# Another order of the 32 blocks in layers 1 to 3 of a sparse graph network

## The chip, the cores and the metric

The kernel runs on one core of one Trainium2 chip. The metric is the device time of one execution in microseconds. The core has several engines that run side by side, each with its own queue of instructions in program order: TensorE (PE, with its weight loads PEld), VectorE (DVE), ScalarE (ACT), GpSimd (POOL) and SyncE (SP, which here only issues DMAs). Semaphores order them where one needs another's result.

## The reference

Input `x` has 4096 rows of 256 numbers, and `adj` is a 4096 x 4096 matrix of zeros and ones, symmetric, with ones on the diagonal and few others (a row has some ten). Four layers follow one another, each of the form

```
h = relu(layernorm(x));   x = x + attention_l(h, adj)
```

Layer 0 is a graph attention with 4 heads: a row's score for a neighbour is a sum of two scalars behind a leaky ReLU, softmax runs over the neighbours, the values are `h @ W`, and an ELU follows. Layer 1 has one head, and adds `h @ W` too. Layer 2 has 4 heads and a bias. Layer 3 is dot attention with 4 heads, `softmax(q k / 8) v`, over the neighbours. A row needs the rows of all its neighbours, so no row of a layer can be worked on before all rows of the layer before are done, wherever its neighbours stand.

## The kernel before

The first stage (`lists`, some 430 us) reads `adj`, finds each row's neighbours, sorts the rows by their number of neighbours, and writes them to DRAM in that order. From then on the rows stand in 32 blocks of 128, block 0 with the rows of most neighbours. `CAPS[b]` is the number of neighbours, or slots, that block b is given (lines 40 to 43):

```
CAPS = [
    23, 14, 13, 12, 12, 11, 11, 10, 10, 10, 9, 9, 9, 9, 9, 8,
    8, 8, 8, 7, 7, 7, 7, 6, 6, 6, 6, 5, 5, 5, 4, 3,
]
```

They sum to 277. The fallback of `Net`, a dense version behind a test at the end, isn't taken here.

Each layer l reads a table in DRAM, `tab[l]`, with one row for each row of `x`. For a block, POOL issues one indirect DMA for each slot (`fetch`, line 757): 128 rows of the table, one for each partition, into one slot of `s_ring` in SBUF. The ring holds 36 x 512 numbers: 64 slots of 288 in layer 1, 69 of 264 in layer 2, 36 of 512 in layer 3. In layers 2 and 3 a block of odd K takes one slot more.

`layer` (lines 808 to 902) goes through the blocks in the order of the list `order`: `FIRST` in layer 0, `ORDER` in layers 1 to 3. In round i it does this, and each engine gets its part of it in this order:

- `fill(i)` issues the fetches of coming blocks, up to four blocks ahead (`AHEAD`). A block is placed behind the last one in the ring, or at its start, and only if these slots aren't held by a block that is not yet worked off in program order; otherwise filling stops until the next round. In layer 3 it also stops when four blocks are held, and each block brings a load of its own value rows (`s_vself`, line 834) on SP's queue.
- `norm(d)` finishes the layernorm of an earlier block d for the next layer and turns it on PE (line 742).
- `scores(b)` makes the scores of block b = order[i] on DVE and their exponentials on ACT (line 957). It begins at lines 917 and 918 in layers 1 and 2, and at lines 937 and 940 (products and sums over 256 columns for every slot) in layer 3. In layer 1 `mutual` (from line 965) belongs to it.
- `third(e)` finishes the table row of a still earlier block (`advance`: lines 1098 and 1099 for table 2, 1105 to 1115 for table 3, whose DMA is line 1106), and issues what lies in `made`: in layer 3 the output rows of the block of two rounds before, as an indirect DMA on POOL (`send`, line 767).
- `product(d)` multiplies block d's turned rows with the next layer's weights on PE (line 750).
- `weigh(b)` sums the neighbours' values. In layer 1 DVE does it alone, one instruction for each slot (lines 1008 and 1010). In layers 2 and 3 DVE multiplies up to eight slots at once (line 1039), and PE sums two slots in each pair of matmuls with the identity (line 1044; line 1032 for the block's own row where K is even, after line 1024 has halved its weight).
- `settle(c)` adds the sum to `x` and starts the next layernorm: for the block itself in layer 1, for the block of the round before in layers 2 and 3 (lines 1078 and 571 to 587; in layer 3 only lines 1068 and 1069, which make the output row).

After the last round the last blocks are carried through the same steps, without other work beside them. The first fetch of the next layer waits until the last row of its table is written.

`ORDER` before takes blocks from both ends in turn: 0, 31, 1, 30, 2, 29 and so on, with 14, 17, 15, 16 last. `FIRST` begins with 31, 30, 29, 28, 0, and also sets in which order `reload` brings in the rows; it isn't touched.

Of the kernel before, what the change touches and what calls it, by code (L numbers as in the profile page):

```python
# [47 lines left out]

WL = W + TOPK

ORDER = [b for k in range(16) for b in (k, 31 - k)]

FIRST = [31, 30, 29, 28, 0] + [b for k in range(1, 14) for b in (28 - k, k)] + [14]

# [17 lines left out]
class Sparse:  # L72
# [735 lines left out]
    def layer(self, l):  # L808
# [5 lines left out]
        ring = self.ring[:, : slots * wide].rearrange("p (k w) -> p k w", w=wide)  # L814
        order = ORDER if l else FIRST
        todo, held, at = list(order), {}, 0
# [870 lines left out]
```

## Time and profile before

| | us |
|---|---|
| median of 9 runs | 1817.63 |
| lowest and highest run | 1814.46, 1823.91 |
| the profiled execution | 1819.06 |
| its span, first to last instruction | 1817.3 |
| first fetch of layer 0 | 431.18 |
| first fetch of layers 1, 2, 3 | 643.15, 1014.03, 1388.92 |
| last fetch of layer 3 begins | 1789.72 |
| last send of layer 3 begins | 1811.69 |

| engine | busy us | share of the span |
|---|---|---|
| DVE | 1384.8 | 76% |
| POOL | 1185.4 | 65% |
| PE | 982.1 | 54% |
| ACT | 423.9 | 23% |

The profile is one execution. A row of its timeline gives the start in us, the duration in us, the engine, the line of the kernel, the operation with the tile that it writes and those that it reads, and, in brackets, how long the engine stood idle before it and what ended that. [...] The fetches are known to a block by counting: the order of the blocks is in the code, and K fetches belong to each. In layer 1 the form of line 965 tells the block's K (its second size is 23 x K), and in layers 2 and 4-head scores generally line 918's second size is 4 x K.

### The profile page before, as it was taken

What the parts mean: (1) busy time and instruction counts of PE and PEld (TensorE: products, weight loads), DVE (VectorE), ACT (ScalarE), POOL (GpSimd) and SP (SyncE); (2) the same over time, 40 slices, a digit from 0 to 9 for tenths busy, and PEclk for the clock granted to TensorE, in tenths of its full rate; (3) what the DMA queues carried; (4) which work ended last, traced back from release to release, by engine and by line L of the source; (5) the groups of instructions that cost most, each with busy time, mean ns of one, the idle gap of its engine ahead of it and who ended that gap; (6) DMA issues with size and microseconds to landing.
All of it is one profiled execution on the core that took longest, in us unless ns stands there. A gap on an engine that the chain in (4) does not pass through costs nothing. (4 is left out here: it accounts for less than half of the span.)

```text
span 1817.3 us, 14342 instructions
## 1 busy us (share of the span) xinstructions
PE 982.1 (54%) x2551; PEld 473.5 (26%) x2551; DVE 1384.8 (76%) x3900; ACT 423.9 (23%) x1240; POOL 1185.4 (65%) x1324
## 2 busy tenths in 40 slices
PE   4877877752576602223222167788684354454455
PEld 2523323221454401111111033334341121121112
DVE  6888999952689808888888168888885587887886
ACT  5864434101244401111111012222221000000000
POOL 1067756676666267777776577777773577776774
PEclk9988989875688955555555589899987676677777
DMA  9899887347633144444444345454444577775773
GB/s 329 279 395 336 303 276 253 102 140 243 187 98 95 46 102 123 133 130 132 130 132 113 74 119 137 131 135 133 134 131 124 154 214 208 207 208 176 210 203 112
DMA packets 123017, 312.89 MB, mean 172 GB/s; under 512 B 31236, under 2 KB 49671, under 8 KB 122920
## 3 DMA queue, kind: packets, MB, share of 16 engines
q0 software_dynamic: 68064, 207.46, 40.9%
q1 hardware_dynamic: 54856, 104.44, 16.6%
q14 instruction: 73, 0.60, 0.1%
q8 instruction: 24, 0.39, 0.1%
HBM read 276.80 MB, written 35.00 MB: 172 GB/s over the span
## 5 line engine op out<-in xcount | busy, mean ns | idle before, releaser
L757 POOL DMA_INDIRECT s_ring<-s_tab,s_near x924 | 883.8, 956 | 348.0 <-issue 185.6
L1044 PE MATMUL s_acc<-s_ring,s_ident 128*128 128x512 f32 x588 | 313.0, 686 | 184.2 <-issue 93.3
L757 POOL DMA_INDIRECT s_g<-s_tab,s_keep x192 | 183.1, 954 | 64.4 <-issue 58.0
L1044 PEld LDWEIGHTS s_acc<-s_ring,s_ident 128*128 128x128 f32 x588 | 127.5, 223 | 363.7 <-issue 242.2
L485 DVE MAX8 s_cand<-s_pt 128x8 f32<-128x256 f32 x512 | 181.8, 417 | 17.7 <-PE s_pt L483 17.3
L1039 DVE TENSOR_TENSOR s_ring<-s_ring,s_shares 128x2048 f32<-128x2048 f32 (+7 forms) x121 | 187.5, 1573 | 0.0
L742 PE MATMUL s_pht<-s_ident,s_h 128*128 128x128 f32 x128 | 34.4, 361 | 250.2 <-ACT s_h L734 250.1
L750 PE MATMUL s_ps<-s_we_l,s_ht 128*128 128x264 f32 x256 | 114.7, 592 | 93.0 <-ACT s_ht L744 93.0
L1010 DVE SCALAR_TENSOR_TENSOR s_acc<-s_ring,s_p,s_acc 128x256 f32<-128x256 f32 x277 | 135.7, 490 | 9.7
L263 ACT ACTIVATE s_low<-s_raw 128x1024 fp8e4<-128x1024 int32 x128 | 134.2, 1049 | 22.6 <-DMA s_raw<-in_adj_dram 19.7
L558 PE MATMUL s_ae<-s_g,s_ident 128*128 128x512 f32 x192 | 116.1, 701 | 37.2 <-DVE s_g L549 37.2
L478 PE MATMUL s_pt<-s_low,s_mark 128*128 128x512 fp8e4 x256 | 108.7, 425 | 32.5 <-DVE s_cand L485 12.8
L577 ACT ACTIVATE s_y<-s_mv,s_eps 128x1 f32<-128x1 f32 x96 | 28.3, 294 | 390.3 <-DVE s_mv L572 390.3
L750 PE MATMUL s_ps_kv<-s_wkv,s_ht 128*128 128x512 f32 x128 | 80.7, 763 | 67.1 <-ACT s_ht L744 67.1
L937 DVE TENSOR_TENSOR s_ring<-s_ring,s_shares 128x2048 f32<-128x2048 f32 (+7 forms) x48 | 81.1, 1690 | 36.2 <-DMA s_ring<-s_tab,s_near 35.7
L483 PE MATMUL s_pt<-s_places,s_stands 128*128 128x512 bf16 x256 | 107.5, 420 | 1.4 <-DVE s_stands L455 1.4
L957 ACT ACTIVATE s_shares<-s_e 128x32 f32<-128x32 f32 (+8 forms) x87 | 17.5, 201 | 376.7 <-DVE s_e L950 376.7
L918 DVE TENSOR_TENSOR s_e<-s_ring,s_rx 128x8 f32<-128x8 f32 (+12 forms) x87 | 15.8, 181 | 113.9 <-DMA s_ring<-s_tab,s_near 109.7
L750 PEld LDWEIGHTS s_ps<-s_we_l,s_ht 128*128 128x128 f32 x256 | 63.8, 276 | 124.0 <-ACT s_ht L744 114.0
L742 PEld LDWEIGHTS s_pht<-s_ident,s_h 128*128 128x128 f32 x128 | 18.1, 172 | 291.3 <-ACT s_h L734 279.8
L940 DVE TENSOR_REDUCE s_e<-s_ring 128x32 f32<-128x2048 f32 (+7 forms) x48 | 81.2, 1692 | 1.7
L502 POOL TENSOR_SCALAR s_ids<-s_top 128x23 f32<-128x23 f32 x32 | 10.1, 314 | 108.6 <-DVE s_top L493 108.3
(195 smaller groups left out, 1690.2 us busy)
## 6 DMA issues: line engine op xcount, KB each, us to landing
s_raw<-in_adj_dram SPq DMA_DIRECT2D x128, 512.0 KB, 8.3
s_ring<-s_tab,s_near POOLq DMA_INDIRECT x924, 3.0
s_rx<-s_placed SPq DMA_DIRECT2D x32, 262.0 KB, 7.3
s_tab<-s_kv SPq DMA_DIRECT2D x32, 256.0 KB, 2.9
s_tab<-s_keep SPq DMA_DIRECT2D x8, 528.0 KB, 7.7
s_tab<-s_rx SPq DMA_DIRECT2D x32, 132.0 KB, 2.1
s_keep<-in_x_dram SPq DMA_DIRECT2D x8, 512.0 KB, 8.3
s_vself<-s_tab SPq DMA_DIRECT2D x32, 128.0 KB, 3.6
```

The lines of the kernel that those rows point to most:

```text
L263: nc.scalar.activation(low[r][:, ts(h, n // 4)], raw.pop(q), AF.Copy, saturate=False, accum_out=self.sums[:, r, h : h + 1],)
L478: nc.tensor.matmul(pt, lhsT=self.mark, rhs=lo[:, ts(g, IB)], start=True, stop=False)
L483: nc.tensor.matmul(pt, lhsT=self.stands[:, g, :], rhs=self.places, start=False, stop=True)
L485: nc.vector.max(out=cand[:, g * (IB // CH) + k, :], in_=pt[:, ts(k, CH)])
L558: nc.tensor.matmul(acc, lhsT=self.ident, rhs=g[:, :, k, 0:D], start=False, stop=(k == E - 1))
L750: self.nc.tensor.matmul(ps[:, :width], lhsT=ht[:, c, :], rhs=w[:, c, :], start=(c == 0), stop=(c == KC - 1),)
L757: return self.nc.gpsimd.indirect_dma_start(out=out, out_offset=None, in_=table[:, :], in_offset=bass.IndirectOffsetOnAxis(ap=idx, axis=0),)
L937: nc.vector.tensor_tensor(kq, kq, q.unsqueeze(1).to_broadcast([P, m, D]), ALU.mult)
L940: nc.vector.tensor_reduce(e[:, k0 : k0 + m, :], kq.rearrange("p k (h d) -> p k h d", h=4), AX.X, ALU.add)
L1010: nc.vector.scalar_tensor_tensor(acc, g[:, k, 0:D], p[:, k, :], acc, ALU.mult, ALU.add)
L1039: nc.vector.tensor_tensor(v, v, p[:, k0 : k0 + m, :].unsqueeze(3).to_broadcast([P, m, H, D // H]), ALU.mult)
L1044: nc.tensor.matmul(both, lhsT=self.ident, rhs=g[:, k : k + 2, v0 : v0 + D], start=(k == 0 and not full), stop=(k + 2 >= K),)
```

## The change

The list `ORDER` is replaced. Nothing else is changed.

```
-ORDER = [b for k in range(16) for b in (k, 31 - k)]
+
+ORDER = [0, 1, 2] + [b for k in range(3, 15) for b in (30 - k, k)] + [15, 28, 29, 30, 31]
+assert sorted(ORDER) == list(range(32))
```

Layers 1, 2 and 3 now take blocks 0, 1, 2 first (23, 14 and 13 slots), then 27, 3, 26, 4, 25, 5 and so on down to 16, 14, and at the end 15, 28, 29, 30, 31 (8, 5, 5, 4 and 3 slots). The first block is the same. Layer 0 keeps its order.

## The prediction, made before the changed kernel was run

> **What bounds the kernel now.** I read the table of busy time by stage, then POOL's timeline where each layer begins and ends, then DVE's waits by layer, then DVE's timeline for single blocks. All ahead of 643 us uses FIRST and stays. First the stages, one row each for the fetches of layers 1, 2 and 3:
>
> ```profile
> core 0: us, PE busy (x) PEld busy (x) DVE busy (x) ACT busy (x) POOL busy (x), PEclk, DMA share, GB/s
> 643.00:992.00 349.00, 84.47 (x180) 43.92 (x180) 274.07 (x935) 50.27 (x182) 264.02 (x277) 0.50 0.49 128
> 1014.00:1364.00 350.00, 247.10 (x600) 119.34 (x601) 256.94 (x747) 75.56 (x261) 265.09 (x277) 0.87 0.49 128
> 1389.00:1791.00 402.00, 186.03 (x306) 71.37 (x306) 306.17 (x436) 21.40 (x91) 290.20 (x304) 0.72 0.68 198
> ```
>
> No engine is at 9 tenths, yet 277 fetches take 349 us: each needs 0.95 us and 0.30 us of issue, 1.257 us in all, and in layers 1 and 2 they stand without a hole. POOL's timeline at the ends of layers 1 and 2:
>
> ```profile
> 990.34 0.95 POOL L757 DMA_INDIRECT s_ring<-s_tab,s_near  x1 [0.30 <-issue]
> 1014.03 0.95 POOL L757 DMA_INDIRECT s_ring<-s_tab,s_near  x1 [22.74 <-DMA s_tab<-s_rx]
> ...
> 1362.30 0.95 POOL L757 DMA_INDIRECT s_ring<-s_tab,s_near  x1 [0.30 <-issue]
> 1388.92 0.95 POOL L757 DMA_INDIRECT s_ring<-s_tab,s_near  x1 [25.67 <-DMA s_vself<-s_tab]
> ```
>
> So a layer is 277 fetches and a drain of 22.7 or 25.7 us, in which DVE finishes what it has in hand and the last table rows are written. The order decides what DVE has in hand. DVE's waits, layer 1 and then layer 2:
>
> ```profile
> DVE s_e L918 <- DMA s_ring<-s_tab,s_near: 37.8, 1, 37.8
> ...
> DVE s_e L918 <- DMA s_ring<-s_tab,s_near: 59.0, 17, 36.1
> ```
>
> In layer 1 DVE waits once for a fetch, for block 0, and never again: from 677.2 to 1007 it is the slower of the two. In layer 2 it waits 17 times, so it is level with POOL. What a block costs DVE is read from one block's start to the next's (L965 in layer 1; L917 in layer 2):
>
> ```profile
> 736.54 0.33 DVE L965 TENSOR_SCALAR s_eq<-s_ring,s_own_f 128x115 bf16<-128x115 f32 x1
> 744.80 0.36 DVE L965 TENSOR_SCALAR s_eq<-s_ring,s_own_f 128x276 bf16<-128x276 f32 x1
> ...
> 987.56 0.31 DVE L965 TENSOR_SCALAR s_eq<-s_ring,s_own_f 128x184 bf16<-128x184 f32 x1
> 997.45 0.31 DVE L965 TENSOR_SCALAR s_eq<-s_ring,s_own_f 128x184 bf16<-128x184 f32 x1
> ...
> 1119.39 0.15 DVE L917 TENSOR_TENSOR s_e<-s_rx 128x4 f32<-128x4 f32 x1
> 1127.70 0.16 DVE L917 TENSOR_TENSOR s_e<-s_rx 128x4 f32<-128x4 f32 x1
> ```
>
> A block of 5 slots costs DVE 8.26 us in layer 1 and 8.31 in layer 2; POOL fetches it in 5 x 1.257 = 6.3. A block of 8 costs 9.9 against 10.1: level. So small blocks burden DVE, large ones POOL, and their place in the order matters.
>
> **The change, part by part.** No instruction is added or removed: the same 831 fetches, matmuls and vector operations are issued, only permuted, those on SP too (the table writes and the loads of s_vself follow their blocks).
>
> *Layer 1, the end.* Now the last five blocks are 15, 28, 29, 30, 31 with 8, 5, 5, 4, 3 slots. Before, small blocks early gave DVE a store of work; with 0, 1, 2 first (50 fetches) and the small ones last, it runs dry. Without a wait DVE would reach block 14 at 34.0 (its start in the layer) + 330.2 (all its blocks, 677.2 to 1007.4) - 51.8 (the last six) = 312.4 us into the layer; block 14 lands at 252 x 1.257 + 2.0 = 318.8. So it waits there, and then holds the end: blocks 14, 15, 28, 29, 30 cost 10.6 (9 slots, 967.02 to 977.58) + 9.9 + 8.3 + 8.3 + 7.7 (4 slots, 716.13 to 723.82) = 44.7 us, while POOL fetches the 25 slots after block 14 in 31.4. Block 31 begins 13.3 us after it landed; block 16 now begins 4.2 after (landed 993.2, begun 997.4). That is +9.1; the last block itself costs 7.1 (3 slots, 695.75 to 702.83) in place of 9.9, -2.8. **Sum +6.3 us.** Bounds: 3 if the drain hides half, 9 if the 2.8 is lost on PE or ACT.
>
> *Layer 2, the end.* DVE is at its landing when block 15 comes. Blocks 15, 28, 29, 30 cost 9.4 (8 slots, 1355.20 to 1364.45 and 0.13 to L918) + 8.3 + 8.3 + 8.2 (4 slots, 1078.72 to 1086.93) = 34.2 us; POOL's 17 fetches take 21.4. Block 31 begins 12.8 after landing; block 16 began 0.2 after: +12.6. Its own chain is shorter: L1039 0.95 in place of 2.28, L1024 gone (0.2), a wait of 0.96 for PE before L1078 gone: -2.5. **Sum +10.1.** Four small blocks in a row are not in this trace. Bounds: 5, half of it, since each small block stands beside a large one now and some of its 8.3 may be theirs; and 25, if PE becomes the limit (rival three).
>
> *Layer 3, the beginning.* Its ring has 36 slots. Blocks 0 and 31 fill 28; block 1 waits until PE has read block 0:
>
> ```profile
> 1420.37 0.95 POOL L757 DMA_INDIRECT s_ring<-s_tab,s_near  x1 [0.30 <-issue]
> 1434.82 0.95 POOL L757 DMA_INDIRECT s_ring<-s_tab,s_near  x1 [13.50 <-PE s_acc L1044]
> ```
>
> The instant 1434.82 hangs on block 0 alone and stays. But block 31's three fetches, done under that wait now, are to be done later: +3.8.
>
> *Layer 3, the middle.* I walked fill() through both orders. The old one has two rounds (after blocks 8 and 9) in which nothing fits, so two rows of output are sent back to back, and the second waits until the first has landed:
>
> ```profile
> 1635.53 0.99 POOL L767 DMA_INDIRECT out_dram<-s_out,s_near  x1 [0.30 <-DVE s_me L1025]
> 1640.09 0.98 POOL L767 DMA_INDIRECT out_dram<-s_out,s_near  x1 [3.57 <-DVE s_out L1068]
> ```
>
> These cost 3.57 and 3.29 where 0.30 is usual. The new order has a fill in every round from the first to the 29th: -6.3. Sends ahead of the last fetch are 26 in both.
>
> *Layer 3, the end.* From the last fetch's end to the last send's end it is now 22.0 us (1790.67 to 1812.66). After the change, block 15's fetch ends 26.5 us ahead of the last (17 fetches, 4 sends of 1.285); it starts 4.1 later, as now; then DVE spends 11.3 (8 slots) + 7.5 + 7.5 + 7.0 + 4.9 on the five blocks, 0.9 on block 30's sum, some 2 for PE, 0.9 and 1.2 for the last sum and send: 20.5. So -1.5. **Layer 3 sums to -4.0.** Bounds -10 (the two holes and all of the short drain) and +6 (a second wait for the ring at block 3, as long as half of the first).
>
> In sum 6.3 + 10.1 - 4.0 = +12.4 us. The profiled execution took 1819.06 us (span 1817.3), 1.4 above the median of 1817.63; the sum gives 1831.5 for it, and **1830 us** against the median.
>
> [...] In layer 3's drain a matmul of 512 columns took 1.02 us after an idle of 5.54 us and 0.47 us in dense stretches, and the granted clock is 0.50 in layer 1, 0.87 in layer 2. [...]
>
> **The rivals.** *One, faster: the short last block wins.* If DVE kept up with the small blocks, every drain would only lose slots: -2.8, -2.5 and -4.0, or -9.3: 1808 us. It decides from the point at which 5 slots cost DVE less than POOL's 6.3 us; the measured 8.3 speaks against it. *Two, no change:* DVE's total in layer 1 does not depend on the order, so if its store of work outlasts the large blocks, layer 1 gives 0, layer 2 gives its lower bound 5, layer 3 gives -4: 1819. The 6.4 us between 312.4 and 318.8 speak against it. *Three, slower still: PE at half clock.* Block 30's matmuls in layer 2 fill 0.4 + 2.0 + 1.0 + 1.0 + 1.9 = 6.3 us of its 8.2; twice that is 12.6, and four blocks would cost 4.4 more each: +17.6 on the forecast, 1848. The clock of 0.87 speaks against it; half of it would still give 1839.
>
> **How the numbers follow.** Forecast 0.66 (1822 to 1839), rival three 0.14, rival two 0.12, rival one 0.08. The range of 1820 to 1842 takes in the forecast, half of rival three and the edge of rival two. Faster by over 0.2% (3.6 us, about what a measurement of this kernel can tell from no change): 0.08; within: 0.12; slower: 0.80.
>
> **What would show it.** Right: the 277 fetches of layers 1 and 2 still take 348 us without a hole; the drains after them grow from 22.7 to about 29 and from 25.7 to about 36; DVE begins block 31 about 13 us after its landing; POOL's first hole in layer 3 is 17 us, and no send in its middle waits 3 us. Wrong: drains that shrink (rival one), or matmuls of about 1 us in layer 2's last 40 us (rival three), or a second hole of POOL in layer 3.

## The result, and the profile after

The changed kernel took a median of 1830.50 us (10 runs, 1826.89 to 1834.33) against 1817.87 us of the kernel before (31 runs): a ratio of 1.0070, 95% interval 1.0058 to 1.0082. It is slower, by about the size forecast (1830).

The profiled execution took 1831.40 us (span 1829.6). In all that follows a layer's length is the time from its first fetch to the next layer's (for layer 3 to the end of its last send), and its drain is the part after its last fetch. All ahead of layer 1 is unchanged, but it ended 2.74 us earlier in this execution.

| us | before | after | difference | forecast |
|---|---|---|---|---|
| first fetch of layer 1 | 643.15 | 640.41 | -2.7 | 0 |
| length of layer 1 | 370.87 | 377.70 | +6.8 | +6.3 |
| length of layer 2 | 374.90 | 388.08 | +13.2 | +10.1 |
| length of layer 3 | 423.74 | 418.73 | -5.0 | -4.0 |
| end of the last send | 1812.66 | 1824.92 | +12.3 | +12.4 |

The last row agrees with the forecast to 0.1 us, and that is luck: the three layers together grew by 15.0 us, 2.6 more than forecast, and the shorter part ahead of layer 1 hides it.

POOL's timeline of the changed kernel at the ends of layers 1 and 2 (the fetch is line 759 now; the number in brackets ahead of a layer's first fetch is the drain):

```profile
987.77 0.95 POOL L759 DMA_INDIRECT s_ring<-s_tab,s_near  x1 [0.30 <-DVE s_y L580]
1018.11 0.95 POOL L759 DMA_INDIRECT s_ring<-s_tab,s_near  x1 [29.39 <-DMA s_tab<-s_rx]
...
1367.31 0.95 POOL L759 DMA_INDIRECT s_ring<-s_tab,s_near  x1 [0.30 <-PE s_acc L1046]
1406.19 0.95 POOL L759 DMA_INDIRECT s_ring<-s_tab,s_near  x1 [37.93 <-DMA s_vself<-s_tab]
```

The fetches themselves still take 348.3 and 350.1 us without a hole. The loss is nearly all in the drains: 29.39 for 22.74, and 37.93 for 25.67 (+6.65 of +6.83, and +12.26 of +13.18). Why they are longer shows in DVE's timeline of layer 1's end, line 920 being the second instruction of each block (the form 128x9 is block 14, then 15, 28, 29, 30, 31):

```profile
960.38 0.17 DVE L920 TENSOR_TENSOR s_e<-s_ring,s_rx 128x9 f32<-128x9 f32 x1 [1.83 <-DMA s_ring<-s_tab,s_near]
...
971.00 0.17 DVE L920 TENSOR_TENSOR s_e<-s_ring,s_rx 128x8 f32<-128x8 f32 x1
...
980.73 0.17 DVE L920 TENSOR_TENSOR s_e<-s_ring,s_rx 128x5 f32<-128x5 f32 x1
...
988.84 0.17 DVE L920 TENSOR_TENSOR s_e<-s_ring,s_rx 128x5 f32<-128x5 f32 x1
...
996.89 0.17 DVE L920 TENSOR_TENSOR s_e<-s_ring,s_rx 128x4 f32<-128x4 f32 x1
...
1004.28 0.15 DVE L920 TENSOR_TENSOR s_e<-s_ring,s_rx 128x3 f32<-128x3 f32 x1
```

DVE waits for block 14 (1.83 us), so at that point it has no work in store. The five blocks then take 10.62, 9.73, 8.11, 8.05 and 7.39 us, while POOL's last fetch ends at 988.72: DVE begins the last block 15.6 us later. Before, it began its last block 6.1 us after the last fetch. In layer 2 the last block's row, after and before (last fetches end at 1368.26 and 1363.26), shows the same: 15.4 us later, where it was 2.0:

```profile
1383.68 0.16 DVE L920 TENSOR_TENSOR s_e<-s_ring,s_rx 128x12 f32<-128x12 f32 x1
...
1365.29 0.19 DVE L918 TENSOR_TENSOR s_e<-s_ring,s_rx 128x32 f32<-128x32 f32 x1 [0.68 <-DMA s_ring<-s_tab,s_near]
```

DVE's waits for fetches in layer 1, and then in layer 2, total, times and longest:

```profile
DVE s_e L920 <- DMA s_ring<-s_tab,s_near: 45.7, 8, 38.4
...
DVE s_e L920 <- DMA s_ring<-s_tab,s_near: 77.5, 17, 36.7
```

They were 37.8 and 59.0. In layer 1 this is nearly a whole account: length less waits is 333.1 us before (370.87 - 37.8) and 332.0 after, so DVE's work is the same and the layer grows by what DVE waits, less 1.1. In layer 2 it is not: the waits grow by 18.5 us and the layer by 13.2. In layer 3 POOL's first hole, ahead of block 1:

```profile
1433.86 0.95 POOL L759 DMA_INDIRECT s_ring<-s_tab,s_near  x1 [0.30 <-issue]
1451.90 0.95 POOL L759 DMA_INDIRECT s_ring<-s_tab,s_near  x1 [17.09 <-PE s_acc L1046]
```

17.09 for 13.50; but the waits of 3.57 and 3.29 ahead of sends in the middle are gone, the fetch stretch is 2.6 shorter (399.1 for 401.7) and the tail 2.4 shorter (19.6 for 22.0).

### The profile page after: what moved, and what is told of

The parts are those of the page before. It is cut to its first block, busy times and chain, and to the rows that moved or that the text cites. A ratio compares the mean times of both kernels' runs of the same rounds, so it can differ in the third digit from the quotient of the medians.

```text
span 1829.6 us, 14358 instructions
## 1 busy us (share of the span) xinstructions
PE 980.7 (54%) x2551; PEld 470.9 (26%) x2551; DVE 1383.9 (76%) x3900; ACT 425.0 (23%) x1240; POOL 1186.7 (65%) x1324
## 5 line engine op out<-in xcount | busy, mean ns | idle before, releaser
L480 PE MATMUL s_pt<-s_low,s_mark 128*128 128x512 fp8e4 x256 | 108.0, 422 | 33.6 <-DVE s_cand L487 13.8
L920 DVE TENSOR_TENSOR s_e<-s_ring,s_rx 128x8 f32<-128x8 f32 (+13 forms) x87 | 16.1, 185 | 140.3 <-DMA s_ring<-s_tab,s_near 136.4
L504 POOL TENSOR_SCALAR s_ids<-s_top 128x23 f32<-128x23 f32 x32 | 10.1, 315 | 107.2 <-DVE s_top L495 106.9
```

The lines of the kernel that those rows point to most:

```text
L480: nc.tensor.matmul(pt, lhsT=self.mark, rhs=lo[:, ts(g, IB)], start=True, stop=False)
```

## The experiments

The theory: the four small blocks at the end cost DVE some 8 us each against 5 or 6 of POOL, DVE has no store of work left to cover this, and so the drains of layers 1 and 2 grow. Rivals: the large blocks at the head make the loss (POOL alone is at work there); or PE, at half clock, sets the pace of the small blocks.

Not all chips on which the experiments ran gave the same time for the unchanged kernel: 1816 to 1818 us on some, as above, and 2170 us on others. Every ratio is against the kernel before on the same chip, taken over the runs and not from the two medians, and the two groups stand apart here.

### On chips where the kernel before takes 1817 us

**Both kernels again**, unchanged. Run e6 is before, e7 after.

> The kernel before, unchanged, for its trace under the conditions of the experiments. In the runs e1 to e5 it took about 2170 us, not 1818, and the traces of those kernels showed DVE standing idle for 0.5 to 1.9 us between its instructions while POOL issues fetches. Theory (on these chips DVE, not POOL, is the limit of layers 1 and 2): where it takes 2170 us, layers 1, 2 and 3 are about 503, 467 and 474 us long, with POOL halted for want of ring slots in layers 1 and 2; where it takes 1818 us, 371, 375 and 424, as in the profile shown, with no halt of POOL there. Rival (the whole program is slower, fetches too): the fetches stand more than 1.26 us apart even where POOL is not halted.

> The changed kernel, unchanged, on the same chip. If the chip takes 1818 us for the kernel before: +12.5 us (1.007), as in the result; layer 1 +7, layer 2 +13, layer 3 -5. If it takes 2170 us: the sum of the pieces found there, the tail alone +6 and +7 in layers 1 and 2, the head alone +5 and +7.5, and layer 3 by itself +2.5, that is between +13 (the pieces overlap) and +28 (they add). Rival (the result holds only where POOL is the limit): below +5 at 2170 us.

Before took 1816.46 (11 runs; profiled 1817.31), after 1834.68 (7 runs): ratio 1.0096, interval 1.0072 to 1.0121. Lengths of layers 1, 2, 3: before 370.4, 375.3, 422.8; after 377.3, 385.1, 418.5. So +6.9, +9.7 and -4.3: the three differences return, and layer 2 now stands where the forecast put it. Their sum is +12.3; the median is 18.2 up, and the expected ratio of 1.007 lies just under the interval. The profiled execution of e7 took 1823.70, the fastest of the seven, and its part ahead of layer 1 was 5.9 us shorter than in e6. In which part the other six executions were longer than this one no trace shows.

**The tail alone** (this is the kernel of e1, whose expectation stands further below):

```
-ORDER = [b for k in range(16) for b in (k, 31 - k)]
+ORDER = [b for k in range(14) for b in (k, 27 - k)] + [28, 29, 30, 31]
```

> The kernel of run e1 (0, 27, 1, 26 ... in turn, and 28, 29, 30, 31 last: the tail of the change without its head), for a chip on which the kernel before takes about 1818 us, as in the profile shown and in run e6. Theory (the four small blocks at the end, at 8 us of DVE each against 6.3 of POOL, make the drain of layers 1 and 2): layer 1 about 377 us in place of 370.5 (+6 to +7), layer 2 about 385 in place of 375 (+10 to +12), the same as with the whole change; layer 3 between 415 and 420; together +8 to +14. Rival (the three large blocks at the head make the loss, since DVE has nothing to do for 22 us in more than one place): layers 1 and 2 within 2 us of the old order. If the chip takes 2170 us: as in run e1, 1.004 to 1.008.

1833.08 against 1816.01, ratio 1.0086 (1.0072 to 1.0100). Its POOL timeline at the two ends:

```profile
1020.58 0.95 POOL L757 DMA_INDIRECT s_ring<-s_tab,s_near  x1 [29.47 <-DMA s_tab<-s_rx]
...
1406.52 0.95 POOL L757 DMA_INDIRECT s_ring<-s_tab,s_near  x1 [36.50 <-DMA s_vself<-s_tab]
```

The lengths are 377.7, 385.9 and 421.6. Layers 1 and 2 lose as much with the tail alone as with the whole change (377.3 and 385.1 in e7), and DVE waits 46.2 us for fetches in layer 1, 45.7 with the whole change. So the head costs nothing there. In layer 3 the tail alone gives only -1.3 of the -4.3; the rest comes with the head. This is a miss: 415 to 420 us were expected there, and +8 to +14 us in all, where the median is 17.1 up. The rival of the head falls for layers 1 and 2.

**Which engine sets the pace: a dose of idle work** in the changed kernel.

```
@@ weigh, layer 1
-            nc.vector.tensor_scalar(acc, me, p[:, K, :], None, ALU.mult)
+            for _ in range(5 if b in (28, 29, 30) else 1):
+                nc.vector.tensor_scalar(acc, me, p[:, K, :], None, ALU.mult)
@@ advance, layer 2 (times does its matmuls n times)
-            ps = self.times(ht, self.wkv, 2 * D, f"kv{name}")
+            ps = self.times(ht, self.wkv, 2 * D, f"kv{name}", n=2 if b in (14, 15, 28) else 1)
```

> The changed kernel with idle work added in two places; the output stays the same. In layer 1 DVE's first product of blocks 28, 29 and 30 (0.49 us, 0.52 from one to the next) is done five times: 2.1 us more of DVE in each. In layer 2 PE's product with the weights of the next layer, the first two thirds of it (four matmuls, 1.98 us at full clock), is done twice for blocks 14, 15 and 28: 2 us more of PE in each. Theory (DVE alone sets the pace of the small blocks; PE has over 2 us of slack in each): layer 1 +6.2 us over the changed kernel (377.5 to 383.7), layer 2 unchanged, 385 to 388. Rival three of the prediction (PE is or is near the limit of the small blocks of layer 2): layer 2 +4 to +6, 390 to 394. Rival (the round trip of a block through ACT and PE sets the pace, DVE only waits inside it): layer 1 less than +2.

1837.48 against 1816.01, ratio 1.0104 (1.0082 to 1.0126). DVE's dose in one block of layer 1, PE's in one block of layer 2, and the two ends, from the timelines of DVE, PE and POOL:

```profile
986.73 2.58 DVE L1011 TENSOR_SCALAR s_acc<-s_rx,s_p 128x256 f32<-128x256 f32 x5
```

```profile
1379.67 3.70 PE L752 MATMUL s_ps_kv<-s_wkv,s_ht 128*128 128x512 f32 x8 [0.93 <-ACT s_ht L746]
```

```profile
1027.89 0.95 POOL L759 DMA_INDIRECT s_ring<-s_tab,s_near  x1 [35.64 <-DMA s_tab<-s_rx]
...
1413.30 0.95 POOL L759 DMA_INDIRECT s_ring<-s_tab,s_near  x1 [35.75 <-DMA s_vself<-s_tab]
```

In layer 1, 2.1 us more of DVE in three blocks make the layer 383.8 for 377.3 in e7, that is +6.4 (6.2 expected): every us put on DVE comes out at the end. In layer 2, 1.7 us more of PE (eight matmuls in 3.70 for four in 1.98) beside three blocks make it 385.4 for 385.1: nothing. Products that were slow by themselves cost nothing there either: the one beside block 29 took 3.38 us in e7 for 1.98, and block 29 took 8.2 us (8.3 in the profile before). So DVE sets the pace of the small blocks, and PE has at least 1.7 us of slack beside each. A whole block at half clock (6.3 us more of PE, the author's estimate from block 30's 6.3 us), on which the price of rival three rests, no run shows.

**A version from the theory**, an order for each layer:

```
+SECOND = [31, 1, 30, 2, 29, 0] + [b for b in ORDER if b not in (31, 1, 30, 2, 29, 0)]
+LAST = [27, 26, 0] + turns([b for b in range(1, 31) if b not in (26, 27)]) + [31]
-        order = ORDER if l else FIRST
+        order = (FIRST, SECOND, ORDER, LAST)[l]
```

(`turns` takes from the front and the back of its list in turn.)

> A version made from the theory, an order for each layer. Layer 1: 31, 1, 30, 2, 29, 0 and then the old order, so that DVE has work after 3 fetches instead of 23; layer 2: the old order; layer 3: 27, 26, 0 first, which fill the 36 slots of the ring to the last, then large and small in turn, 31 last. If the chip takes 1818 us for the kernel before: layer 1 -2.5 (DVE is only 19 us behind POOL at the end, and most of that is the last block itself), layer 3 about -18, together about 1798. If it takes 2170 us (DVE the limit of layer 1): DVE starts up to 25 us earlier, layer 1 -10 to -25, layer 3 about -13 as in the run e5, together about -23 to -38. Rival (how early DVE starts does not matter): layer 1 within 1.5 us of the old order on either chip.

1802.81 against 1816.46, ratio 0.9918 (0.9893 to 0.9944): faster than both kernels, though less than expected (1798). All of it is layer 3: 405.6 for 422.8, and no fetch of it waits over 2 us, where one waited 12.87 in e6. Layer 1 is a miss, 371.4 for 370.4. DVE's waits there say why:

```profile
DVE s_e L931 <- DMA s_ring<-s_tab,s_near: 38.7, 4, 17.4
```

DVE starts after 3 fetches, but waits in four places instead of one, 38.7 us in all for 37.4 in e6. A small block first only splits the wait.

### On chips where the kernel before takes 2170 us

First what is different there, since it decides how the runs count. DVE and POOL in layer 1 of run e3 (whose layers 1 and 2 have the order of before):

```profile
815.15 0.49 DVE L1011 SCALAR_TENSOR_TENSOR s_acc<-s_ring,s_p,s_acc 128x256 f32<-128x256 f32 x1 [0.22 <-DVE s_acc L1009]
816.55 0.49 DVE L1011 SCALAR_TENSOR_TENSOR s_acc<-s_ring,s_p,s_acc 128x256 f32<-128x256 f32 x1 [0.91 <-DVE s_acc L1011]
817.95 0.49 DVE L1011 SCALAR_TENSOR_TENSOR s_acc<-s_ring,s_p,s_acc 128x256 f32<-128x256 f32 x1 [0.91 <-DVE s_acc L1011]
```

```profile
814.82 0.96 POOL L758 DMA_INDIRECT s_ring<-s_tab,s_near  x1 [0.31 <-issue]
816.08 0.96 POOL L758 DMA_INDIRECT s_ring<-s_tab,s_near  x1 [0.30 <-issue]
817.34 0.96 POOL L758 DMA_INDIRECT s_ring<-s_tab,s_near  x1 [0.30 <-issue]
...
847.94 0.96 POOL L758 DMA_INDIRECT s_ring<-s_tab,s_near  x1 [14.52 <-issue]
```

An instruction of DVE takes the same 0.49 us and a fetch the same 1.26, but in this stretch DVE begins one instruction in 1.40 us (0.52 in e6, where seven take 3.64 us). DVE falls so far behind that the ring fills and POOL halts for 14.5 us at 833. Its 277 fetches, busy for 264.54 us, are spread over 434 us of layer 1, where it is 264.58 in 349 us in e6; in layer 2 it is 265.58 in 394 us for 265.89 in 350. So there it is DVE, and not POOL, that sets the pace. Layers 1 and 2 are some 503.5 and 467 us long there with the order of before (mean of e3 and e5).

**The tail alone, the head alone, 31 alone moved to the end, and the change in layer 3 only.** The edit of e1 stands above; the others are

```
e2: ORDER = [0, 1, 2] + [b for k in range(3, 17) for b in (34 - k, k)] + [17]
e4: ORDER = [b for k in range(16) for b in (k, 31 - k) if b != 31] + [31]
e3: NEW = the changed order;  order = (FIRST, ORDER, ORDER, NEW)[l]
```

> The order is (0, 27, 1, 26, ... 13, 14) and then 28, 29, 30, 31, in layers 1 to 3: the small blocks at the end without the three large ones in front. Theory (a block of 3 to 5 slots costs DVE 7 to 8.3 us and POOL only 3.8 to 6.3, so a backlog of DVE grows at the end): layer 1 takes 7 us more than before, layer 2 12 more, layer 3 about 2 less (five fetches of block 27 lie under the first wait in place of three, but three rounds fill nothing), in all 1835 us. Rival head (the large blocks in front starve DVE and cause the loss): layers 1 and 2 as before, 1816. Rival short end (a last block of 3 slots shortens each drain): 1809.

> The order is 0, 1, 2 and then (31, 3, 30, 4, ... 18, 16), 17, in layers 1 to 3: the three large blocks in front, the end level as before. Theory: layers 1 and 2 as before to within 1 us; layer 3 waits for its ring 17 us in place of 13.5 and still has two rounds that fill nothing: 3.8 more, in all 1822. Rival head: layers 1 and 2 take some 6 and 12 more, 1838.

> The old order, but block 31 (3 slots) is taken from the second place and put last, in layers 1 to 3. Theory: after block 16 DVE needs 9.9 us where POOL needs 3.8, so block 31 starts about 6 us after landing in layer 2: layer 1 takes 1 more, layer 2 4 to 5 more, layer 3 3 more (block 31's fetches are no longer under the first wait), in all 1826. Rival short end: 2.8 and 1.1 us less in layers 1 and 2, with layer 3's 3 more 1817; without it 1813.

> Layers 1 and 2 keep the old order, layer 3 alone has the new one. Theory: layers 1 and 2 as before (370.9 and 374.9 us from first fetch to first fetch), layer 3 from its first fetch to the end of its last send 418.7 in place of 423.7: 5 less, in all 1813. Rival: layer 3's gain comes from what layer 2's end leaves behind (PE's clock, queues), and not from its own order: layer 3 as before, 1818.

| run | us, before on that chip | ratio (95%) | layer 1, layer 2 |
|---|---|---|---|
| e1, tail | 2183.60, 2170.68 | 1.0059 (1.0035 to 1.0084) | 509.6, 473.8 |
| e2, head | 2188.57, 2170.68 | 1.0082 (1.0051 to 1.0112) | 508.4, 474.5 |
| e4, 31 last | 2189.08, 2170.68 | 1.0100 (1.0064 to 1.0135) | 507.0, 480.4 |
| e3, layer 3 only | 2173.13, 2170.68 | 1.0021 (0.9996 to 1.0046) | 504.3, 467.3 |

The tail costs 6 and 7 us here too (7 and 12 were expected), but the head, for which the theory says nothing, costs 5 and 7.5, and e4 3.5 in layer 1 and 13.5 in layer 2, where 1 and 4 to 5 were expected. e3 was to gain 5 us (the figure for a chip of 1817 us), and its interval leaves that out. These are misses. The theory is one of a POOL and a DVE that are level, and here they are not; these runs do not test it, and what makes their costs no run shows.

**The head alone once more, and the dose the other way round** (PE in layer 1, DVE in layer 2). Both fell to chips of this group.

```
e12: @@ advance, layer 1:  ps = self.times(ht, self.we2, W, name, n=3 if b in (14, 15, 28) else 1)
     @@ weigh, layer 2:    for _ in range(5 if l == 2 and b in (28, 29, 30) else 1):  the product of the own values
```

> The kernel of run e2 (0, 1, 2 first, then 31, 3, 30, 4 ... in turn to 18, 16, 17: the head of the change without its tail), for a chip on which the kernel before takes about 1818 us. Theory (the head alone costs nothing in layers 1 and 2, because the small blocks come in between, where DVE is behind or level anyway): layers 1 and 2 within 2 us of the old order (370.5 and 375); layer 3 between 418 and 424 (the hole at the ring 16.5 in place of 13, its middle without the two waits of 3 us); together -5 to +3. Rival (the head, not the tail, is what the change costs): layers 1 and 2 +5 or more each, as run e2 showed at 2170 us. If the chip takes 2170 us: as in run e2, 1.005 to 1.011.

> The changed kernel with the idle work of run e11 the other way round; the output stays the same. In layer 1 PE's product for blocks 14, 15 and 28 is done three times (2.13 us each, half clock): 4.3 us more of PE in each. In layer 2 DVE's product of the own values of blocks 28, 29 and 30 (0.42 us) is done five times: 1.4 to 1.8 us more of DVE in each. Theory (DVE alone sets the pace of the small blocks): layer 1 unchanged, 377 to 378; layer 2 +4 to +5.5 over the changed kernel (385 to 388), 389 to 393.5. Rival (PE or the round trip through ACT and PE sets the pace): layer 1 +4 or more, layer 2 less than +2.

The head gave 2192.86 against 2170.67, ratio 1.0097 (1.0068 to 1.0126), lengths 511.3 and 475.4: run e2 once more. So the head alone was never measured at 1817 us; there its cost follows only by difference, from e9 and e7. Run e12 gave 2204.72, ratio 1.0161 (1.0123 to 1.0199); the changed kernel has no run of its own on such a chip, so its lengths can't be set against it. One stretch can be read: in the drain of layer 2, where POOL is done and DVE runs almost without those gaps (idle for no more than 0.41 us at a time), blocks 28, 29 and 30 take 10.1, 10.4 and 9.9 us (from 1668.28 to 1698.69). Without the dose, in e7, blocks 29 and 30 take 8.2 and 8.1. So 1.8 us more of DVE (five products in 2.24 us for one in 0.42) make a block 1.8 to 2.2 us longer in layer 2 too.

**An order that fills the ring of layer 3**, the `LAST` of run e8 in layer 3 alone:

> Layers 1 and 2 keep the old order. Layer 3 alone takes 27, 26 (6 ring slots each), then 0 (24 slots), which fill the ring's 36 exactly, then large and small in turn, and 31 last. Theory (in layer 3 POOL's fetches set the pace, and the wait for the ring behind block 0 is pure loss): on a chip where the kernel before takes 1818 us, POOL's first hole shrinks from 13.5 us to under 2, since DVE and PE have read the first slots of block 0 and blocks 27 and 26 long before their places are wanted; layer 3 from first fetch to the end of the last send takes some 405 us in place of 423.7, in all 1799. Rival: the hole only moves (DVE becomes the limit once POOL doesn't wait, as its 319 us busy of 429 suggest with its waits for PE and ACT): layer 3 stays within 4 us of 423.7, 1816.

2158.04 against 2170.39, ratio 0.9950 (0.9932 to 0.9968). The sign is as expected on this chip too: 12.4 us less, where layer 3 of e8 was 17.2 us shorter at 1817 (18 expected).

## Why the prediction was right, step by step

*What bounds the kernel.* Right. Layers 1 and 2 remain 277 fetches without a hole and a drain, and DVE's work in hand at the last fetch is the drain.

*Layer 1, the end: +6.3 forecast, +6.8 measured.* Both terms hold. A fetch lands 3.1 us after its row of 0.95 us begins (median of 924; 3.0 in the profile before), for the 2.0 us after its end in the sum. DVE begins its last block 13.5 us after its landing (990.8; forecast 13.3), and from that beginning to the next layer's first fetch it is 13.8 us (1004.28 to 1018.11) for 16.7 before: -2.8, as forecast. The five blocks took 43.9 us for the 44.7 of the sum. What was not right is the place of the waits: the 6.4 us were all put at block 14, and the trace has seven waits of 0.25 to 1.83 us spread over the layer (45.7 - 38.4 = 7.3 us), of which block 14's is 1.83.

*Layer 2, the end: +10.1 forecast, +13.2 measured.* The later start was right: DVE begins the last block 15.4 us after the last fetch's end for 2.0, so +13.4, and 13.4 after its landing at 1370.24 (forecast 12.8). The mis-sized term is "its own chain is shorter", forecast at -2.5: 22.5 us for 23.6, so -1.1. The fetch stretch adds 0.9. Two products of PE, one in either profile, explain why the chain gained so little. The first is in the profile of the changed kernel: the last block's first product, and below it the same in run e7 of the same kernel:

```profile
1398.99 3.68 PE L752 MATMUL s_ps_kv<-s_wkv,s_ht 128*128 128x512 f32 x4 [1.58 <-ACT s_ht L746]
```

```profile
1393.30 1.98 PE L752 MATMUL s_ps_kv<-s_wkv,s_ht 128*128 128x512 f32 x4 [1.66 <-ACT s_ht L746]
```

The same four matmuls take 3.68 us in one execution and 1.98 in the other, and DVE waits 4.2 us for them instead of 2.5. With 1.98 the chain is 20.9 us in e7 and e9 and 20.8 in e11. The second is in the profile before, from which the forecast was made: the product of block 17, with DVE's wait behind it, and then the same product in run e6:

```profile
1368.86 3.35 PE L750 MATMUL s_ps_kv<-s_wkv,s_ht 128*128 128x512 f32 x4 [2.71 <-ACT s_ht L744]
...
1377.73 0.88 DVE L1078 TENSOR_TENSOR s_rx<-s_rx,s_acc 128x256 f32<-128x256 f32 x2 [0.96 <-PE s_acc L1044]
```

```profile
1369.13 1.98 PE L750 MATMUL s_ps_kv<-s_wkv,s_ht 128*128 128x512 f32 x4 [3.04 <-ACT s_ht L744]
```

In e6, where it takes 1.98, DVE does not wait ahead of L1078, and the chain is 22.5 us for 23.6. So the "wait of 0.96 for PE before L1078" in the forecast's term belonged to that one execution and not to the old order. Where both kernels ran these products in 1.98 us the chain is 1.6 to 1.7 us shorter, close to the 1.33 of L1039 and the 0.2 of L1024. Between the two profiles the slow product of the one (1.1) and that of the other (1.6) leave -1.1 of it: -1.6 - 1.1 + 1.6.

That is the mechanism of rival three, in one place and not in each block. Its sign, matmuls of about 1 us in layer 2's last 40 us, did appear (3.68 us for four, with a granted clock of 0.54 from 1398.99 to 1402.67), but it cost 1.6 us and not 17.6, and the profile before has it too (3.35 us, with 0.57 from 1368.86 to 1372.21). The granted clock in the profile of the changed kernel, in the 8 us ahead of the 3.68 and then from its start through the next product:

```profile
core 0: us, PE busy (x), PEclk, DMA share, GB/s
1391.00:1399.00 8.00, 4.43 (x15) 1.00 0.17 66
...
1399.00:1403.50 4.50, 4.50 (x8) 0.62 0.00 0
```

The length of PE's idle time just before does not tell which of the two it will be: ahead of the 3.68 PE stood idle for no more than 1.58 us at a time in these 8 us, while the longer gap of 3.04 us in e6 was followed by 1.98. What sets it no run shows. In e7 the product of block 15 took 3.38 after an idle of 2.43 without making its block longer (8.2 us); in the last block, where nothing is left beside it, the lower clock showed in the time.

*Layer 3: -4.0 forecast, -5.0 measured.* The hole at the ring grew by 3.6 (forecast 3.8), the fetch stretch as a whole shrank by 2.6 (forecast -2.5), since the back-to-back sends are gone, and the tail shrank by 2.4 (forecast -1.5; the terms given for it add up to 20.8 and not 20.5, which would be -1.2). No second hole appeared at block 3.

*The rivals.* One (the short last block wins): the shorter last block is real, -2.8 in layer 1, but the blocks of 5 slots cost DVE 8.1 us, not less than POOL's 6.3, and run e11 shows that DVE's time in them comes out at the end. Two (no change): its condition, a store of work that outlasts the large blocks, is not met, since DVE waits eight times where it waited once. Three (PE at half clock): what there was of it is hidden by the slack of PE beside the small blocks (run e11), but for the last block.

Still open: why six of the seven executions of e7 took longer than the profiled one, by 9.3 to 14.5 us, and so why its ratio (1.0096) lies above the first one (1.0070); and what the head costs by itself at 1817 us.

## What to carry to other kernels

Where a loop feeds one engine from another, write down for each size of piece what it costs either engine: here DVE's cost of a block has a large part that does not depend on its slots (8.1 us at 5 slots, 9.7 at 8), POOL's has none (1.26 us a slot). Small pieces last then lengthened the drain, though the very last piece was shorter. And the order that is right for one stage need not be right for the next: the gain of run e8 came from an order for layer 3 alone, made for the size of its ring.

## What the runs showed of the hardware that was not expected

The same program took 1817 us on some chips and 2170 us on others. A sum of DVE over 256 columns (line 1010 of the kernel before) lasts 0.49 us and a fetch follows another after 1.26 us on both; what differs is idle time of DVE between its instructions. Groups of DVE instructions in the window 720 to 990 us of run e3 (2170 us) and of run e6 (1817 us), busy time and mean ns of one, then the idle time before them:

```profile
L970 DVE TENSOR_REDUCE s_has<-s_eq 128x5 f32<-128x115 bf16 (+8 forms) x13 | 5.0, 382 | 33.6 <-remote 28.8 <-issue 4.6
```

```profile
L969 DVE TENSOR_REDUCE s_has<-s_eq 128x9 f32<-128x207 bf16 (+8 forms) x27 | 9.5, 354 | 0.9
```

It is the same line of the kernel. On the one chip DVE stands idle for 33.6 us before 13 of these sums (5.45 us before the one at 835.45); on the other for 0.9 us before 27.

It is tempting to put this down to POOL's issuing, since in the drain of layer 2 in e12, where POOL has nothing to issue, DVE runs almost without the gaps (0.41 us at most) on a chip of 2170 us too. The trace of e3 does not bear that out. From 833.4 to 847.9 POOL is halted there, and DVE still stands idle in it, for up to 3.09 us at a time; then POOL issues a fetch every 1.26 us again from 847.94 on, and DVE does fourteen products beside it at 0.52 us each:

```profile
844.58 0.16 DVE L1000 RECIPROCAL s_t<-s_t 128x1 f32<-128x1 f32 x1 [3.09 <-issue]
...
846.71 7.31 DVE L1011 SCALAR_TENSOR_TENSOR s_acc<-s_ring,s_p,s_acc 128x256 f32<-128x256 f32 x14
```

So the gaps are not simply those of POOL's issuing. What holds DVE up, and what differs between the chips, no run shows.
